# Row halves for the products with C, one fixed PSUM tile, and the step-size sums issued later, in an adaLN Mamba-2 block

## The chip, the cores and the metric

The kernel runs on one core of one Trainium2 chip. A core has a matrix engine (TensorE, PE in the profile; its weight loads are PEld), a vector engine (VectorE, DVE), an activation engine (ScalarE, ACT), a general engine (GpSimd, POOL) and a queue engine that issues transfers (SyncE, SP). The metric is the device time of one execution in microseconds (us). Matrix products accumulate in PSUM, eight banks of 2 KB per partition; a bank holds 128 x 512 numbers of 32 bits. All numbers are float32, and TensorE makes such a product in two passes, which the profile counts as two instructions.

## The reference, cut to what matters

Four sequences of 512 tokens with 512 features go through a normalized Mamba-2 block and a feed-forward layer with binarized weights. Both are modulated and gated by a vector c.

```python
h = layernorm(x) * (1 + ca) + sa
xBCzA = einsum('bld,ed->ble', h, in_proj_w)     # 2048 conv channels, 1024 z, 64 step sizes
xBC = silu(conv1d(xBC, width 4) + bias)         # x: 1024, B: 8 x 64, C: 8 x 64
dt = softplus(A_log); x_in = x / dt
# chunks of 128 tokens, 64 heads of 16, 8 groups of 8 heads, state 64
Y_diag = einsum('bcshn,bczhn,bhcsz,bczhp->bcshp', C, B, exp(segsum(-dt)), x)
states = einsum('bcshn,bhcs,bcshp->bchpn', B, decay_to_end, x)   # and a scan over chunks
Y_off = einsum('bcshn,bchpn,bhcs->bcshp', C, states_before, exp(cumsum(-dt)))
y = (Y_diag + Y_off + D * x_in) * silu(z + z_bias)
x = x + ga * (y @ out_proj.T)
h = layernorm(x) * (1 + cb) + sb
x = x + gb * (h @ binarized(ffn).T + ffn_b)
```

## The kernel before

The 2048 tokens are worked in eight halves of 256 tokens (two halves per sequence). A half has two chunks of 128 tokens (c) and four pairs of groups (gp), so eight units (h, c, gp), 64 in all. Every chunk but a sequence's first reads a state (48 units), and every chunk but its last makes one for the next (48 units).

The loop at the end of the program goes unit by unit. In a step it issues the exponentials of the unit ahead (`stage1`), then the pieces of other work that the lists FRONT and the tails put into that step, then the products of the step's own unit (`stage2`), and the loads of the decay sums for the unit after the next (`stage0`). A scheduler then sets each engine's order from the order of the program, priorities and its own estimate of when operands are there. A tile pool gives each tile a buffer; a tile that finds none free waits for the last reader of the oldest one.

FRONT spreads the work on half h over the eight steps of half h-1: load and normalize x, transpose it (`f_hT`), the step sizes (`f_dt`), then pairs of 128-channel projections for B, C and x in the order B0, C0, x0, x1, B1, C1, x2, x3, and z behind them. A pair (`conv_pair`, L367 to L391) is: four accumulating matmuls per tile into a PSUM buffer "mm" (names pp_B, pp_C, pp_x), a scaled copy on ScalarE (L379), three multiply-adds on VectorE per tile for the convolution (L383), one tanh on ScalarE (L387), and one last multiply on VectorE (L391). For C the last multiply is two, over 64 partitions each: group 0 of a pair goes to partitions 0 to 63 and the first 256 columns of each zeroed block `cd`, group 1 to partitions 64 to 127 and the other columns. So `cd` is block-diagonal, and one full-array matmul of 256 columns serves both groups of a pair.

B and x are then transposed to tokens by TensorE (L399, pt_bt and pt_xt, four transposes each) into PSUM buffers "tr", and copied by ScalarE (L418, L428). `f_dt` makes the 128 x 128 step sizes on VectorE, and behind them products with triangular matrices (pe L330 and L331, pc L344), exponentials and copies of them (sh L346, es), transposes (pn L353, pr L359), and three writes to DRAM (sums_d, e_d, r_d), from which later loads spread the values over partitions.

For a unit, `stage1` multiplies B with C (pg L509, masked into gm on VectorE L511), takes 16 exponentials on ScalarE (L516, 128 x 128 each) and multiplies them with gm (L519, twice 128 x 1024). `stage2` makes state times C (L543, 48 units), then 16 heads as column strips (L549): eight strips for each group r, of 32 output columns each, four side by side on the array, two accumulated. VectorE adds the two (L557, L558, or L561 in first chunks), GpSimd adds the skip term and multiplies with z (L559, L562). Products with B transposed (pst L574) update the state (L579, L584).

The tail of a chunk is the output projection (po L606), a layer norm, four transposes (ph L621), the feed-forward product (pf L634) and the output. PSUM is divided as: mm four banks, tr two, g one (pg), y one (py).

## Time and profile before

| what | before |
|---|---|
| time, median of three runs | 829.75 us (828.38 to 831.42) |
| profiled execution, its own time | 828.1 us |
| its span | 826.4 us |
| granted TensorE clock, mean | 0.980 |
| TensorE busy | 773.7 us, 5008 matmul passes |
| VectorE, ScalarE, GpSimd busy | 647.4, 529.2, 258.2 us |
| exponentials L516 | 1024, 313.8 us on ScalarE |
| decay products L519 | 128, 168.4 us on VectorE |
| writes of cd L391 | 32, 29.0 us on VectorE |
| products pg L509 and py L543 | 128 and 96 passes, 43.8 and 28.9 us busy on TensorE |

Of the page, the first part gives each engine's busy time, and the second cuts the span into 40 slices with the busy share in tenths. Matmuls are pipelined and overlap in the records, so the sum of their durations is more than the time they take; the time that one takes is better read from the start of one to the start of the next. The view of waits lists what an engine stood still for: the waiting instruction's tile and line, what it waited for, the total, how often and the longest.

### The profile page before, as it was taken

The numbers are of one execution on the slowest core, as the hardware profiler recorded it, in microseconds if no ns is written. First come the engines' busy times: TensorE is split into PE (matmuls) and PEld (weight loads), VectorE is DVE, ScalarE is ACT, GpSimd is POOL, SyncE is SP. The second block draws the span as 40 slices with busy tenths as digits, with TensorE's granted clock in tenths as the row PEclk, the third lists the DMA queues.
The fourth block names the chain that finished last, engine by engine and source line by source line (L and its number), as shares of the span: only waits on it lengthen the run. The fifth ranks groups of instructions, "written<-read, shape, count | busy, mean of one in ns | idle before, by whom it ended". The sixth has DMA issues, their size and how long they took to land. (4 is left out here: it accounts for less than half of the span.)

```text
span 826.4 us, 14794 instructions
## 1 busy us (share of the span) xinstructions
PE 773.7 (94%) x5008; PEld 531.7 (64%) x5008; DVE 647.4 (78%) x1249; ACT 529.2 (64%) x1510; POOL 258.2 (31%) x293
## 2 busy tenths in 40 slices
PE   5979889999999999999999999999999999999875
PEld 0853657767667767667667767667667766667431
DVE  3688779995899669995899669996899768995742
ACT  0455485677667778577767678476758687676640
POOL 5020312353223412353223412253213521353431
PEclk9979999999999999999999999999999999999986
DMA  8856542525344372425444272344434382343620
GB/s 297 324 136 199 148 103 68 136 62 137 94 116 127 87 180 68 129 70 128 103 112 133 74 190 68 104 94 104 128 101 113 91 204 52 113 103 90 147 58 13
DMA packets 120139, 99.26 MB, mean 120 GB/s; under 512 B 73976, under 2 KB 98552, under 8 KB 120064
## 3 DMA queue, kind: packets, MB, share of 16 engines
q1 hardware_dynamic: 120064, 98.32, 44.9%
q8 instruction: 40, 0.66, 0.4%
q14 instruction: 35, 0.29, 0.1%
HBM read 92.50 MB, written 5.79 MB: 119 GB/s over the span
## 5 line engine op out<-in xcount | busy, mean ns | idle before, releaser
L516 ACT ACTIVATE decay<-decay,st 128x128 f32<-128x128 f32 x1024 | 313.8, 390 | 39.5 <-DMA decay<-sums_d 39.0
L519 DVE SCALAR_TENSOR_TENSOR decay<-decay,gm 128x1024 f32<-128x1024 f32 x128 | 168.4, 1322 | 11.4 <-ACT decay L516 10.6
L367 PE MATMUL pp_x<-hT,win 128*128 128x259 f32 x512 | 124.5, 393 | 3.4 <-DVE u_B L383 3.4
L606 PE MATMUL po<-wout,z 128*128 128x512 f32 x256 | 122.0, 615 | 5.3 <-POOL z L562 5.3
L367 PE MATMUL pp_z<-hT,win 128*128 128x256 f32 x512 | 115.1, 379 | 0.0
L367 PEld LDWEIGHTS pp_x<-hT,win 128*128 128x128 f32 x512 | 95.6, 193 | 23.0 <-issue 7.7
L367 PEld LDWEIGHTS pp_z<-hT,win 128*128 128x128 f32 x512 | 95.4, 189 | 15.7 <-issue 3.3
L549 PE MATMUL py<-decay,xpad 128*32 128x128 f32 x2048 | 81.8, 280 | 6.6 <-DVE decay L519 5.4
L383 DVE SCALAR_TENSOR_TENSOR u_x<-pp_x,cw,u_x 128x256 f32<-128x256 f32 x192 | 81.8, 476 | 2.2 <-ACT u_x L379 1.7
L442 POOL TENSOR_TENSOR xs<-u_x,rr 128x512 f32<-128x512 f32 x32 | 47.2, 1474 | 112.7 <-DVE u_x L391 68.1
L606 PEld LDWEIGHTS po<-wout,z 128*128 128x128 f32 x256 | 47.2, 194 | 51.6 <-issue 44.1
L549 PEld LDWEIGHTS py<-decay,xpad 128*32 128x32 f32 x2048 | 54.1, 111 | 36.0 <-issue 23.8
L569 POOL TENSOR_TENSOR xd<-xpad,ed 128x256 f32<-128x256 f32 x48 | 35.2, 732 | 131.4 <-PE pst L574 101.8
L562 POOL TENSOR_TENSOR z<-yt,z 128x256 f32<-128x256 f32 x64 | 66.7, 1042 | 30.4 <-DVE yt L561 18.9
L559 POOL TENSOR_TENSOR yt<-yt,xs 128x256 f32<-128x256 f32 x48 | 38.9, 811 | 111.1 <-DVE yt L558 110.9
L634 PE MATMUL pf<-bwT,h 128*128 128x512 f32 x128 | 63.5, 636 | 6.6 <-DVE u_x L383 5.8
L367 PE MATMUL pp_B<-hT,win 128*128 128x259 f32 x256 | 60.6, 382 | 0.0
L367 PE MATMUL pp_C<-hT,win 128*128 128x259 f32 x256 | 58.9, 381 | 0.0
L623 ACT ACTIVATE h<-ph,modT 128x128 f32<-128x128 f32 x64 | 24.5, 456 | 48.7 <-PE ph L621 48.7
L451 ACT ACTIVATE uz<-pp_z,zb 128x256 f32<-128x256 f32 x64 | 26.9, 466 | 43.7 <-PE pp_z L367 41.7
L367 PEld LDWEIGHTS pp_B<-hT,win 128*128 128x128 f32 x256 | 47.5, 190 | 11.2 <-issue 4.3
L367 PEld LDWEIGHTS pp_C<-hT,win 128*128 128x128 f32 x256 | 48.4, 190 | 7.4
(129 smaller groups left out, 1083.3 us busy)
## 6 DMA issues: line engine op xcount, KB each, us to landing
decay<-sums_d SPq DMA_DIRECT2D x128, 256.0 KB
decay<-sums_d SPq DMA_DIRECT2D x128, 128.0 KB
rr<-r_d SPq DMA_DIRECT2D x64, 128.0 KB
wm<-in_w_mod SPq DMA_DIRECT2D x24, 256.0 KB
e<-e_d SPq DMA_DIRECT2D x96, 64.0 KB
x<-in_x SPq DMA_DIRECT2D x16, 256.0 KB
win<-in_w_inT SPq DMA_DIRECT2D x4, 1024.0 KB
xr<-in_x SPq DMA_DIRECT2D x16, 256.0 KB
```

The source lines that it names most:

```text
L367: mm(pm, win[:, k, col : col + P], H[h]["hT"][:, k, lo:], start=(k == 0), stop=(k == NK - 1))
L383: nc.vector.scalar_tensor_tensor(u[:, j, :], pm[:, k : k + T], cw[:, t, k : k + 1], u[:, j, :], ALU.mult, ALU.add)
L442: nc.gpsimd.tensor_tensor(xs, xc, rr, ALU.mult)
L451: nc.scalar.activation(u[:, q, :], pm[:, q, :], AF.Identity, bias=zb[:, 2 * j + q : 2 * j + q + 1], scale=0.5)
L516: nc.scalar.activation(ets[r][:, i, :], ets[r][:, i, :], AF.Exp, bias=H[h]["st"][:, hd : hd + 1])
L519: nc.vector.scalar_tensor_tensor(ets[r], ets[r], 1.0, bc_mid(gm[:, r, :], HPG), ALU.min, ALU.mult)
L549: mm(py[32 * j : 32 * j + 32, 0, r, :], xp[:, r * 2 * P + 32 * i : r * 2 * P + 32 * i + 32], ets[r][:, i, :], start=(q == 0), stop=(q == 1))
L559: nc.gpsimd.tensor_add(t, t, xs)
L562: nc.gpsimd.tensor_mul(zg, t, zg)
L569: nc.gpsimd.tensor_tensor(xd, xg, by_head(H[h]["ed"][:, hd0 : hd0 + HPP]), ALU.mult)
L606: mm(po, H[h]["z"][g // 2][:, g % 2, c * CH : (c + 1) * CH], wout[:, g, :], start=(g == 0), stop=(g == NKI - 1))
L634: mm(pf, h2[:, k, :], bwT[:, k, :], start=(k == 0), stop=(k == NK - 1))
```

## The change

C is kept once, as a tile of 128 partitions and two blocks of 256 tokens, with no zeros; its last multiply is one instruction over 128 partitions. The two groups of a pair lie on partitions 0 to 63 and 64 to 127, and B times C and state times C become two matmuls each, one on the upper and one on the lower half of the array's rows, of 128 columns.

The outputs with C, the strips and the state update go to one fixed PSUM tile `gy` of twelve runs of 128 columns (three banks): runs 0 and 1, or 5 and 6 for odd gp, hold a unit's strips, 3 and 4 its state output, 8 and 7 B times C, 9 and 10 the state update. All other PSUM tiles, the transposes of B and x and the step-size products among them, share five "mm" banks.

The new function `glued` issues the first of a list of products as it comes, and the others right behind it with high priority. It is used for the eight strips of one group, and for state times C of a unit with B times C of the unit two ahead. `stage0` and `stage1` of a unit are now issued two units ahead, behind `stage2` of the current one.

`f_dt` ends with the step sizes; all that followed (pe, pc, sh, es, pn, st, pr, rh and the three writes) is `f_sums`, which stands behind the first pairs of projections B0 and C0 and is issued after the last matmul of C0. The pools u, th and rr have one buffer more each (3, 2, 2).

```diff
-    ps = ctx.enter_context(tc.tile_pool(name="ps", bufs=4, space=PSUM))
+    ps = ctx.enter_context(tc.tile_pool(name="ps", bufs=5, space=PSUM))
-    cds = []
-    for i in range(3):
-        cd = keep.tile([P, 2, 2, T], F32, name=f"cd{i}")
-        nc.gpsimd.memset(cd, 0.0)
-        cds.append(cd)
+    bgy = ctx.enter_context(tc.tile_pool(name="bgy", bufs=1, space=PSUM))
+    gy = bgy.tile([P, 12, CH], F32, name="gy")
...
+    def f_sums(h):
+        W = 2 * NH
+        ndt, drdt = H[h]["ndt"], H[h]["drdt"]
+        with tc.issue_after(H[h]["last"]):
+            f_sums_products(h, W, ndt, drdt)
...
-        pt = ps.tile([P, 2, 2, P], F32, tag="tr", bufs=2, name=f"pt_{name}")
+        pt = ps.tile([P, 2, 2, P], F32, tag="mm", name=f"pt_{name}")
...
-        cd = cds[(2 * h + q) % 3]
-        conv_pair(
-            h, (DI + NG * NS) // P + 2 * q, f"C{q}",
-            [(cd[r * NS : (r + 1) * NS, :, r, :], slice(r * NS, (r + 1) * NS)) for r in range(2)],
-        )
-        H[h]["C"][q] = cd
+        t = wk.tile([P, 2, T], F32, tag="C", name=f"C_{h}_{q}", bufs=3)
+        conv_pair(h, (DI + NG * NS) // P + 2 * q, f"C{q}", t)
+        H[h]["C"][q] = t
...
+    def glued(products):
+        first = products[0]()
+        with tc.issue_after(first.ins), tc.high_priority(offset=1000):
+            for product in products[1:]:
+                product()
+
+    def by_rows(places, h, c, gp, stationary):
+        return [
+            partial(
+                mm, gy[:, places[r], :], stationary[part],
+                H[h]["C"][gp // 2][part, gp % 2, c * CH : (c + 1) * CH], start=True, stop=True,
+            )
+            for r, part in enumerate((slice(0, NS), slice(NS, P)))
+        ]
+
+    def state_out(h, c, gp):
+        k = (h % HPB) * 2 + c
+        return by_rows((3, 4), h, c, gp, states[h // HPB, k][:, gp, :]) if k > 0 else []
+
+    def b_times_c(h, c, gp):
+        return by_rows((8, 7), h, c, gp, H[h]["B"][gp // 2][:, gp % 2, c * CH : (c + 1) * CH])
...
-        pg = ps.tile([P, 2, CH], F32, tag="g", name=f"pg_{n}", bufs=1)
-        mm(pg, H[h]["B"][gp // 2][:, gp % 2, c * CH : (c + 1) * CH], c_pair(h, c, gp), start=True, stop=True)
-        nc.vector.tensor_mul(gm, pg, bc_mid(upto, 2))
+        nc.vector.tensor_mul(gm, gy[:, 7:9, :], bc_mid(upto, 2))
...
-        py = ps.tile([P, 2, 2, CH], F32, tag="y", name=f"py_{n}", bufs=1)
-        if k > 0:
-            mm(py[:, 1], states[b, k][:, gp, :], c_pair(h, c, gp), start=True, stop=True)
+        lo = 5 * (gp % 2)
+        py = gy[:, lo : lo + 2, :]
...
-            pst = ps.tile([P, P], F32, tag="tr", bufs=2, name=f"pst_{n}")
+            pst = gy[:, 9 + (c * NP + gp) % 2, :]
...
-        (4, f_B, (0,)), (4, f_C, (0,)), (4, f_Bt, (0,)),
+        (4, f_B, (0,)), (4, f_C, (0,)), (4, f_sums, ()), (4, f_Bt, (0,)),
...
+        elif step < len(units):
+            products = state_out(*units[step])
+            for unit in new:
+                products += b_times_c(*unit)
+            if products:
+                glued(products)
+            stage2(*units[step])
+            for unit in new:
+                stage0(*unit)
+                stage1(*unit)
```

More of the change, by code (lines that the diff above doesn't have):

```diff
@@ L1 @@
 from contextlib import ExitStack
+from functools import partial
 import numpy as np
@@ L187, in mod_cols @@
         nc.vector.tensor_scalar(row, pg, 1.0 if t6 in (1, 4) else 0.0, None, ALU.add)
-        pm = ps.tile([P, NK, B], F32, tag="tr", bufs=2, name=f"pm{t6}")
+        pm = ps.tile([P, NK, B], F32, tag="mm", name=f"pm{t6}")
         for dt in range(NK):
@@ L206, in gates_out @@
         grow = wk.tile([B, 3, DM], F32, tag="gates", name="grow", bufs=1)
-        brow = wk.tile([B, DM], F32, tag="th", name="brow", bufs=1)
+        brow = wk.tile([B, DM], F32, tag="th", name="brow")
         nc.sync.dma_start(brow, ffn_b.partition_broadcast(B))
@@ L301, in small @@
             return wk.tile([P, W], F32, tag=tag, name=f"{tag}_{h}", bufs=bufs)
-        pa = ps.tile([P, W], F32, tag="tr", bufs=2, name=f"pa_{h}")
+        pa = ps.tile([P, W], F32, tag="mm", name=f"pa_{h}")
         for c in range(2):
@@ L327, in f_dt, with f_sums_products @@
         )
-        pe = ps.tile([P, 2, W], F32, tag="tr", bufs=2, name=f"pe_{h}")
+        H[h].update(ndt=ndt, drdt=drdt)
+    def f_sums(h):
[3 more added lines that the diff above has]
+            f_sums_products(h, W, ndt, drdt)
+    def f_sums_products(h, W, ndt, drdt):
+        pe = ps.tile([P, 2, W], F32, tag="mm", name=f"pe_{h}")
         mm(pe[:, 0, :], after, ndt, start=True, stop=True)
@@ L340, in f_dt @@
             )
-        pc = ps.tile([NH, 2, 2, CH], F32, tag="tr", bufs=2, name=f"pc_{h}")
+        pc = ps.tile([NH, 2, 2, CH], F32, tag="mm", name=f"pc_{h}")
         for c in range(2):
@@ L350, in f_dt @@
         nc.sync.dma_start(e_d[h], es)
-        pn = ps.tile([P, W], F32, tag="tr", bufs=2, name=f"pn_{h}")
+        pn = ps.tile([P, W], F32, tag="mm", name=f"pn_{h}")
         for c in range(2):
             nc.tensor.transpose(pn[:, c * NH : (c + 1) * NH], sh[:, c, :], ident[:NH, :NH])
-        st = small("st", 2)
+        st = wk.tile([P, W], F32, tag="st", name=f"st_{h}")
         nc.vector.tensor_scalar(st, pn, -1.0, None, ALU.mult)
-        pr = ps.tile([NH, 2, CH], F32, tag="tr", bufs=2, name=f"pr_{h}")
+        pr = ps.tile([NH, 2, CH], F32, tag="mm", name=f"pr_{h}")
         for c in range(2):
@@ L366, in proj @@
         for k in range(NK):
-            mm(pm, win[:, k, col : col + P], H[h]["hT"][:, k, lo:], start=(k == 0), stop=(k == NK - 1))
+            last = mm(pm, win[:, k, col : col + P], H[h]["hT"][:, k, lo:], start=(k == 0), stop=(k == NK - 1))
+        return last.ins
     def conv_pair(h, t0, name, dst=None):
-        u = wk.tile([P, 2, T], F32, tag="u", name=f"u_{name}_{h}", bufs=2)
+        u = wk.tile([P, 2, T], F32, tag="u", name=f"u_{name}_{h}", bufs=3)
         for j in range(2):
@@ L377, in conv_pair @@
             pm = ps.tile([P, KS - 1 + T], F32, tag="mm", name=f"pp_{name}{j}_{h}")
-            proj(pm, h, t * P, 0)
+            H[h]["last"] = proj(pm, h, t * P, 0)
             nc.scalar.activation(
@@ L385, in conv_pair @@
                 )
-        th = wk.tile([P, 2, T], F32, tag="th", name=f"th_{name}_{h}", bufs=1)
+        th = wk.tile([P, 2, T], F32, tag="th", name=f"th_{name}_{h}")
         nc.scalar.activation(th, u, AF.Tanh)
-        if dst is None:
-            dst = [(u, slice(0, P))]
-        for d, r in dst:
-            nc.vector.scalar_tensor_tensor(d, th[r], 1.0, u[r], ALU.add, ALU.mult)
+        nc.vector.scalar_tensor_tensor(u if dst is None else dst, th, 1.0, u, ALU.add, ALU.mult)
         return u
     def to_tokens(src, name):
-        pt = ps.tile([P, 2, 2, P], F32, tag="tr", bufs=2, name=f"pt_{name}")
+        pt = ps.tile([P, 2, 2, P], F32, tag="mm", name=f"pt_{name}")
         for c in range(2):
@@ L403, in f_B @@
         t = wk.tile([P, 2, T], F32, tag="B", name=f"B_{h}_{q}", bufs=3)
-        conv_pair(h, DI // P + 2 * q, f"B{q}", [(t, slice(0, P))])
+        conv_pair(h, DI // P + 2 * q, f"B{q}", t)
         H[h]["B"][q] = t
     def f_C(h, q):
-        cd = cds[(2 * h + q) % 3]
-        conv_pair(
-            h, (DI + NG * NS) // P + 2 * q, f"C{q}",
-            [(cd[r * NS : (r + 1) * NS, :, r, :], slice(r * NS, (r + 1) * NS)) for r in range(2)],
-        )
-        H[h]["C"][q] = cd
+        t = wk.tile([P, 2, T], F32, tag="C", name=f"C_{h}_{q}", bufs=3)
+        conv_pair(h, (DI + NG * NS) // P + 2 * q, f"C{q}", t)
+        H[h]["C"][q] = t
     def f_Bt(h, q):
@@ L432, in f_xt @@
         H[h]["xt"][j] = xp
-        rr = wk.tile([P, 2, T], F32, tag="rr", name=f"rr_{h}_{j}", bufs=1)
+        rr = wk.tile([P, 2, T], F32, tag="rr", name=f"rr_{h}_{j}")
         for r in range(2):
@@ L448, in f_z @@
             proj(pm[:, q, :], h, NCONV + (2 * j + q) * P, KS - 1)
-        u = wk.tile([P, 2, T], F32, tag="u", name=f"uz_{h}_{j}", bufs=2)
+        u = wk.tile([P, 2, T], F32, tag="u", name=f"uz_{h}_{j}", bufs=3)
         for q in range(2):
@@ L453, in f_z @@
             )
-        th = wk.tile([P, 2, T], F32, tag="th", name=f"thz_{h}_{j}", bufs=1)
+        th = wk.tile([P, 2, T], F32, tag="th", name=f"thz_{h}_{j}")
         nc.scalar.activation(th, u, AF.Tanh)
@@ L495, in stage0 @@
         U0[h, c, gp] = (ets, e)
-    def c_pair(h, c, gp):
-        return H[h]["C"][gp // 2][:, gp % 2, :, c * CH : (c + 1) * CH]
+    def glued(products):
[16 more added lines that the diff above has]
+        return by_rows((8, 7), h, c, gp, H[h]["B"][gp // 2][:, gp % 2, c * CH : (c + 1) * CH])
     def stage1(h, c, gp):
@@ L519, in stage1 @@
             nc.vector.scalar_tensor_tensor(
-                ets[r], ets[r], 1.0, bc_mid(gm[:, r, :], HPG), ALU.min, ALU.mult
+                ets[r], ets[r], 1.0, bc_mid(gm[:, 1 - r, :], HPG), ALU.min, ALU.mult
             )
@@ L539, in by_head @@
             return v.rearrange("p (j q) -> p j q", q=2).unsqueeze(3).to_broadcast([P, HPG, 2, HD])
-        py = ps.tile([P, 2, 2, CH], F32, tag="y", name=f"py_{n}", bufs=1)
-        if k > 0:
-            mm(py[:, 1], states[b, k][:, gp, :], c_pair(h, c, gp), start=True, stop=True)
+        lo = 5 * (gp % 2)
+        py = gy[:, lo : lo + 2, :]
         for r in range(2):
-            for q in range(2):
-                for j in range(HPG // 2):
-                    i = 2 * j + q
-                    mm(py[32 * j : 32 * j + 32, 0, r, :], xp[:, r * 2 * P + 32 * i : r * 2 * P + 32 * i + 32],
-                       ets[r][:, i, :], start=(q == 0), stop=(q == 1))
+            glued([
+                partial(
+                    mm, py[32 * j : 32 * j + 32, r, :],
+                    xp[:, r * 2 * P + 32 * (2 * j + q) : r * 2 * P + 32 * (2 * j + q) + 32],
+                    ets[r][:, 2 * j + q, :], start=(q == 0), stop=(q == 1),
+                )
+                for q in range(2) for j in range(HPG // 2)
+            ])
         cs = slice(c * CH, (c + 1) * CH)
@@ L556, in stage2 @@
         if k > 0:
-            nc.vector.tensor_mul(t, py[:, 1], e)
-            nc.vector.tensor_add(t, py[:, 0], t)
+            nc.vector.tensor_mul(t, gy[:, 3:5, :], e)
+            nc.vector.tensor_add(t, py, t)
             nc.gpsimd.tensor_add(t, t, xs)
         else:
-            nc.vector.tensor_add(t, py[:, 0], xs)
+            nc.vector.tensor_add(t, py, xs)
         nc.gpsimd.tensor_mul(zg, t, zg)
@@ L676, in adaln_mamba_block @@
     for step in range(-1, max(steps) + 1):
-        ahead = step + 1 < len(units)
-        late = step < 0 or step % NU == NU - 1
-        if ahead and not late:
-            stage1(*units[step + 1])
         for f, args in steps.get(step, []):
             f(*args)
+        new = units[step + 2 : step + 3] if step >= 0 else units[0:2]
         if step < 0:
-            stage0(*units[0])
-        if 0 <= step < len(units):
+            for unit in new:
+                glued(b_times_c(*unit))
+                stage0(*unit)
[6 more added lines that the diff above has]
+                glued(products)
             stage2(*units[step])
-        if ahead and late:
-            stage1(*units[step + 1])
-        if step + 2 < len(units):
-            stage0(*units[step + 2])
+            for unit in new:
+                stage0(*unit)
+                stage1(*unit)
 _OUT = ((B, L, DM), np.float32)
```

## The prediction, made before the changed kernel ran

> **What bounds the kernel now.** I read the page's busy times and slices first, then TensorE's waits, then windows of 10 us, then the timeline around single projections.

> ```profile
> PE 773.7 (94%) x5008; PEld 531.7 (64%) x5008; DVE 647.4 (78%) x1249; ACT 529.2 (64%) x1510; POOL 258.2 (31%) x293
> PE   5979889999999999999999999999999999999875
> DVE  3688779995899669995899669996899768995742
> ```

> TensorE is the bound from the eighth slice to the 37th. VectorE reaches 9 tenths only in stretches, once per half of 256 tokens.

> ```profile
> engine line waited for: us in total, times, longest us
> PE pf L634 <- DVE u_x L383: 5.8, 3, 1.9
> PE pe L330 <- DVE ndt L322: 3.9, 4, 1.2
> PE pt_bt L399 <- DVE B L391: 1.8, 4, 0.7
> PE py L543 <- DVE yt L558: 1.2, 1, 1.2
> ```

> TensorE's waits in the steady part are few. They name VectorE.

> ```profile
> core 0: us, PE busy (x) PEld busy (x) DVE busy (x) ACT busy (x) POOL busy (x), PEclk, DMA share, GB/s
> 340.00:350.00 10.00, 10.00 (x78) 8.04 (x77) 10.00 (x21) 5.99 (x15) 2.25 (x2) 1.00 0.47 137
> 350.00:360.00 10.00, 10.00 (x73) 7.46 (x72) 9.76 (x24) 8.39 (x24) 6.27 (x9) 1.00 0.42 89
> 380.00:390.00 10.00, 10.00 (x89) 6.83 (x91) 7.45 (x10) 8.34 (x27) 3.05 (x3) 1.00 0.53 130
> ```

> While the next half's projections run (first two windows), TensorE and VectorE are both full; elsewhere TensorE alone is. So a reader of a projection stays unseen only because TensorE has other work in front of what needs it:

> ```profile
> 350.62 4.76 PE L367 MATMUL pp_x<-hT,win 128*128 128x259 f32 x21
> 351.92 0.56 ACT L379 ACTIVATE u_x<-pp_x,cb,cw 128x256 f32<-128x256 f32 x1 [1.19 <-PE pp_x L367]
> 355.16 0.62 ACT L387 ACTIVATE th_x<-u_x 128x512 f32<-128x512 f32 x1
> 355.82 0.69 DVE L391 SCALAR_TENSOR_TENSOR u_x<-th_x,u_x 128x512 f32<-128x512 f32 x1 [0.20 <-ACT th_x L387]
> 356.73 0.66 PE L399 MATMUL pt_xt<-ident,u_x 128*128 128x128 f32 x4
> ```

> The pair x2 of half 3 ends at 351.9. Its first reader (ScalarE) starts then, and the chain's last step on VectorE ends at 356.5, 4.6 us later. The four transposes start at 356.73, and TensorE lost almost nothing, since pp_x3, the state product and a row of strips stood between.

> **The change part by part.**

> The products. Around one unit, before:

> ```profile
> 425.57 0.59 PE L543 MATMUL py<-cd,S 128*128 128x256 f32 x2
> 426.09 1.08 PE L549 MATMUL py<-decay,xpad 128*32 128x128 f32 x32
> 427.10 0.70 PE L509 MATMUL pg<-cd,B 128*128 128x256 f32 x2
> 427.64 0.59 PE L634 MATMUL pf<-bwT,h 128*128 128x512 f32 x1
> ```

> Start to start, a 256-column pass takes 217 ns, a 128-column pass 110, and four column strips together 110. Entering the strips costs 310 instead of 217 (+93); leaving them 202 instead of 109 (+93), and the first full pass behind takes 320 instead of 217 (+104). The 64 L509 and 48 L543 products, two passes each, are 112 x 2 x 217 ns = 48.6 us, and 4.4 us of first-pass surcharges lie on full-array work that goes: -53 us. In their place stand 224 products on row halves, of two 128-column passes. No row of this trace shows two row halves side by side. If they run together as the column strips do: 224 x 110 ns = 24.6 us, and 12.9 us for entering and leaving: +37.5. Strips: they are cut into 104 stretches before (pn, pr and pst stand among them) and 86 after: 92.9 to 86.8 us, -6. Counting every matmul of both instruction orders by these prices (307 mode changes before, 348 after) gives 749.7 and 727.8 us: **-22 us**. If the halves run one after the other, another 24.6 us is due: +2.7. I take -22, by the nearest row (the strips, which share the array), and keep +2.7 as an end.

> [...]

> VectorE: 32 writes of cd (905 ns, 29.0 us) become 16 of 128x512 (u_x's and B's rows: 842 and 750 ns), 13 us: -16 us, two per half. VectorE doesn't end the half, so this is worth nothing by itself; it goes into the lag below. GpSimd loses three memsets of 2.7 us at the start, beside weight loads: nothing.

> The transposes. They move from a PSUM pool of their own into the five "mm" banks, and in the new order stand sooner behind their pair. TensorE work between a pair's end and its transposes, counted with the prices above, in us per half: xt0 8.1-8.9 before, 1.8-3.8 after; xt1 7.7-8.6, then 4.0-4.8; bt1 5.5-7.2, then 4.2-5.3; xt2 4.7-6.8, then 1.2-2.8; xt3 9.3-10.4, then 6.9; bt0 8.7-11.4, then 6.2-7.1. After xt0's pair now come one row group and two strip rows, and pp_x1, which used to cover it, is behind it; xt2 likewise. Over before's pairs, the time from a pair's end to its last VectorE step has a minimum of 4.2 and a median of 7.3 us (bare work: 0.56 + 3 x 0.40 + 0.63 + 0.69 = 3.1). At the minimum xt0 and xt2 each stall (4.2 + 0.15 for the signal) - 2 = 2.4 us: 4.9 per half, 34 us over seven halves. At the other end I walked half 4's new orders on ScalarE and VectorE with the row durations: between the x2 pair and its tanh ScalarE has eight exponentials (2.45 us), VectorE two decay products (1.22 each), yt, gm and S: xt2 stalls 4.75, xt0 2.4, xt1 0.2, and pn 3.4, since the copy of sh now stands behind some ten convolution steps on VectorE, where pn waited for nothing before. 10.8 per half, 75 us. It can't be below nothing: no transpose starts before its data. I take 7.5 per half, **+52 us**, between the two, because VectorE is full in these stretches but catches up while TensorE waits.

> Old stalls. pe (3.9), pf (5.8) and pt_bt (1.8) could go, since VectorE is later relieved and there are more buffers: 0 to -11.5, taken **-9**. What would be late next is the transposes above.

> The step-size sums behind the first projections: pe, pc, pn, pr, their ScalarE and VectorE readers and three DMA writes on SP. The sums are read by the decay loads of the next half's first unit, some three units (about 30 us) on, so the later SP issues cost nothing in the steady part; if that margin went, the exponentials (L516) would start late. In half 0 nothing covers it: pe follows pp_C01 at some 32 us and ndt is there at 36.3, 4.4 us idle, and xt0 and xt1 stall some 3 each: 11 us by 62 us into the span against 5.5 before, **+5** (3 to 8).

> New waits of the glued row group: it waits for gm of the unit before and for yt L557's reading of the state columns, with a whole row of strips queued behind it. The only such wait in the rows is py L543 on yt, once, 1.2 us; gm is made a unit earlier. 0 to 5, taken **+1**. Two units ahead instead of one, u, th and rr with another buffer: they take waits from ScalarE and GpSimd, which aren't the bound: nothing.

> Sum against the profiled execution's own 828.1 us (span 826.4 and 1.7 around it; 1.65 below the median 829.75): 828.1 - 22 + 52 - 9 + 5 + 1 = 855.1, and 856.8 at the median's level: **856**.

> **The rivals.**

> Faster, one mechanism: the lag shrinks to its bare 3.1 us, because VectorE has two us less per half and pauses with TensorE. Then xt0 and xt2 stall 1.1 each, 2 us per half, 16 in all: 828.1 - 22 - 9 + 16 + 3 + 1.65 = 818; with no stall at all 802. It decides where the stalls stay below some 4 us per half. For it: VectorE's share falls in the windows beyond 370 us. Against: no pair of before came below 4.2, and the x2 pair's 4.6 was among the shortest.

> Row halves one after the other: +24.6, some of which stands in front of the transposes and fills their stalls (0.4 per half): 856 + 25 - 3 = 878. For it: no row shows them side by side. Against: strips.

> Shortest lags everywhere: 856 - 18 = 838, the forecast's own lower end.

> **How the numbers follow.** Some 0.3% (2.5 us) can be told from no change. Forecast, with stalls of 34 to 75 us: 0.60, its own range 838 to 880. Faster rival: 0.23. Row halves not together: 0.12. Between 826 and 838, the stalls near 20 us: 0.05. The range that leaves out under 2 in 10 reaches into both: 814 to 884. Faster 0.23, same 0.03, slower 0.74.

> **What would show it.** Row halves: starts of the 64x128 matmuls in pairs some 6 ns apart (strips' spacing), pairs 110 ns apart; else 110 each. Transposes: new waits of TensorE on VectorE's last step for u_x (pt_xt), 2 to 5 us, fourteen or more, and pn on sh. VectorE's total near 631 us; PE's share of the span below 90%. Wrong if pt_xt waits under 1 us on average or the pairs of later halves end in under 4 us.

## The result and the profile after

The changed kernel takes 936.1 us (median of four runs, 930.7 to 937.8), the kernel before 830.6 us beside it: a ratio of 1.126 (95% interval 1.120 to 1.132). The forecast was 856 us, with a range of 814 to 884: the direction was right, the size was not. The profiled execution took 930.74 us, its span is 928.9.

The page of the changed kernel, first and second part, gives busy times and slices:

```profile
PE 791.7 (85%) x5232; PEld 547.9 (59%) x5232; DVE 633.0 (68%) x1233; ACT 533.7 (57%) x1510; POOL 239.5 (26%) x290
PE   4768788889978998979977998979978998989775
DVE  2567758775877569775878559775778559774652
PEclk9879989999989999999979999989989999999977
```

TensorE is busy for 85% of the span instead of 94%, and no other engine is full. The clock row dips all along. That of the kernel before dips at the start and the end only (one stretch of 3.4 us in the middle, at 520 us, is too short to show):

```profile
PEclk9979999999999999999999999999999999999986
```

The waits of TensorE (total, times, longest):

```profile
PE pt_xt L409 <- DVE u_x L401: 31.3, 18, 4.5
PE pn L365 <- DVE sh L358: 17.9, 7, 2.9
PE gy L602 <- DVE yt L586: 12.8, 8, 2.9
PE gy L506 <- DVE gm L537: 10.5, 13, 3.7
PE pe L342 <- DVE ndt L324: 8.4, 5, 4.6
PE gy L602 <- DVE mv_a L259: 7.2, 2, 3.6
PE gy L602 <- DVE yt L589: 5.1, 3, 3.5
PE pt_xt L409 <- DVE mv_a L259: 4.0, 1, 4.0
```

L409 are the transposes of x (35.3 us in all), L365 the transposes of the sums, L602 the state update's product pst (25.1 us: it now waits for its own unit's yt, which is read from the same tile gy), L506 the first of a glued row group, which waits for gm.

One such wait, by the timeline (start, length, and in brackets the idle time before it):

```profile
503.66 0.60 PE L379 MATMUL pp_x<-hT,win 128*128 128x259 f32 x2
504.30 0.56 ACT L392 ACTIVATE u_x<-pp_x,cb,cw 128x256 f32<-128x256 f32 x1 [0.61 <-PE pp_x L379]
504.65 1.22 DVE L545 SCALAR_TENSOR_TENSOR decay<-decay,gm 128x1024 f32<-128x1024 f32 x1
504.76 2.44 ACT L542 ACTIVATE decay<-decay,st 128x128 f32<-128x128 f32 x8
507.35 1.21 DVE L545 SCALAR_TENSOR_TENSOR decay<-decay,gm 128x1024 f32<-128x1024 f32 x1
509.05 0.63 ACT L400 ACTIVATE th_x<-u_x 128x512 f32<-128x512 f32 x1 [1.85 <-DVE u_x L396]
509.72 0.69 DVE L401 SCALAR_TENSOR_TENSOR u_x<-th_x,u_x 128x512 f32<-128x512 f32 x1
510.46 1.12 PE L409 MATMUL pt_xt<-ident,u_x 128*128 128x128 f32 x4 [4.55 <-DVE u_x L401]
511.37 4.64 PE L379 MATMUL pp_x<-hT,win 128*128 128x259 f32 x16
```

The x2 pair ends at 504.2; its chain has eight exponentials and two decay products in its way, as the prediction had walked it, and its transposes start at 510.46, with TensorE idle for 4.55 us (forecast for this place: 4.75). The last line shows what the prediction had no term for: the sixteen projection passes behind the wait take 4.48 us start to start, 280 ns each instead of 217. The windows around it:

```profile
470.00:480.00 10.00, 6.80 (x61) 5.40 (x59) 7.58 (x17) 8.26 (x24) 1.46 (x2) 0.84 0.33 90
480.00:490.00 10.00, 10.00 (x28) 7.02 (x28) 5.47 (x10) 6.38 (x19) 3.25 (x4) 0.70 0.51 122
500.00:510.00 10.00, 5.92 (x68) 4.69 (x60) 9.97 (x22) 6.60 (x18) 1.63 (x3) 1.00 0.47 124
510.00:520.00 10.00, 9.54 (x30) 6.56 (x31) 6.93 (x13) 6.33 (x20) 3.61 (x4) 0.83 0.09 23
```

The number behind the busy times is the granted clock. Behind the waits it is 0.84, 0.70 and 0.83: the record of the clock has stretches at 0.5, mostly of 3.4 or 6.8 us, 28 of them here, 6 before. From 480 to 490 TensorE is busy throughout, while VectorE and ScalarE are busy for 5.47 and 6.38 us of the ten: it is TensorE at its slower clock that holds the kernel there.

The row halves, by the timeline of the same place:

```profile
504.19 0.37 PE L506 MATMUL gy<-C,S 64*128 64x128 f32 x1
504.20 0.37 PE L509 MATMUL gy<-C,S 64*128 64x128 f32 x1
504.40 0.27 PE L506 MATMUL gy<-C,S 64*128 64x128 f32 x1
504.41 0.27 PE L509 MATMUL gy<-C,S 64*128 64x128 f32 x1
504.51 0.39 PE L509 MATMUL gy<-C,B 64*128 64x128 f32 x4
504.83 0.30 PE L506 MATMUL gy<-decay,xpad 128*32 128x128 f32 x1
```

The upper and the lower half start 6 to 8 ns apart in the trace (the view rounds to 10 ns), the second pair some 0.21 us behind the first and each later one some 110 ns behind the one before: they run together. A whole row group (state times C, and B times C) takes from 504.19 to 504.83, 0.64 us, where the two full-array products took 0.52 + 0.54 before.

**Where the time went.** For each run I split the span into TensorE's idle time between its first and last matmul, its busy time, and of that the part lost to the clock (busy time in stretches at clock 0.5, times 0.5); what is left is TensorE's work at full clock. The split is that of the one profiled execution of each kernel; the changed kernel's was its fastest, 930.7 us. The start (8 to 9 us) and the end (4.4) hardly differ.

| kernel | median us | ratio to before (95%) | idle | busy | lost to the clock | work at full clock |
|---|---|---|---|---|---|---|
| before | 830.6 | 1 | 38.8 | 773.7 | 12.4 | 761.3 |
| changed | 936.1 | 1.126 (1.120-1.132) | 124.8 | 791.7 | 53.5 | 738.2 |
| a_sums_back | 978.2 | 1.174 (1.163-1.185) | 147.9 | 815.1 | 78.6 | 736.5 |
| a_pst_mm | 921.4 | 1.106 (1.096-1.116) | 116.7 | 791.0 | 52.6 | 738.4 |
| a_xt_late | 867.7 | 1.041 (1.032-1.051) | 82.6 | 771.5 | 30.6 | 740.9 |
| a_all3 | 905.1 | 1.086 (1.075-1.097) | 110.1 | 782.7 | 45.6 | 737.1 |
| a_fill | 895.4 | 1.076 (1.065-1.086) | 79.3 | 802.1 | 29.0 | 773.1 |
| x_sh | 865.7 | 1.040 (1.024-1.056) | 84.2 | 769.9 | 26.7 | 743.2 |
| x_pn | 865.7 | 1.040 (1.029-1.050) | 83.6 | 768.1 | 25.8 | 742.3 |
| x_pn_bt | 856.0 | 1.028 (1.015-1.042) | 70.5 | 769.9 | 25.1 | 744.8 |
| a_pin_fill | 929.7 | 1.120 (1.116-1.123) | 96.9 | 820.1 | 46.0 | 774.1 |
| a_pin_fill2 | 922.4 | 1.111 (1.109-1.114) | 72.8 | 835.7 | 33.2 | 802.5 |
| b_share6 | 1006.2 | 1.212 (1.208-1.215) | 154.6 | 835.8 | 70.7 | 765.1 |
| a_tr | 854.4 | 1.029 (1.026-1.032) | 66.4 | 772.8 | 23.1 | 749.7 |
| a_gy2 | 805.6 | 0.972 (0.968-0.975) | 37.2 | 752.4 | 12.3 | 740.1 |
| gy2_sums_back | 808.9 | 0.974 (0.973-0.976) | 41.0 | 754.0 | 15.5 | 738.5 |
| gy2_noglue | 810.1 | 0.976 (0.975-0.978) | 38.9 | 758.0 | 12.9 | 745.1 |

From before to the changed kernel: idle +86.0, clock +41.1, work at full clock -23.1, start -1.4, together the 102.5 us of span, but for rounding. The last column is the check on the split: it is 736 to 750 for every kernel with row halves and no fillers, whatever its time, and 761 to 765 without row halves.

### The profile page after: what moved, and what is told of

The parts are those of the page before. It is cut to its first block, busy times and chain, and to the rows that moved or that the text cites. A ratio compares the mean times of both kernels' runs of the same rounds, so it can differ in the third digit from the quotient of the medians.

```text
span 928.9 us, 15115 instructions
## 1 busy us (share of the span) xinstructions
PE 791.7 (85%) x5232; PEld 547.9 (59%) x5232; DVE 633.0 (68%) x1233; ACT 533.7 (57%) x1510; POOL 239.5 (26%) x290
## 4 chain that ended last, share of the span: by engine, by line
PE 60%; DVE 21%; issue 7%; ACT 5%; DMA 4%; POOL 2%; SPq 1%; DVEq 0%; ACTq 0%; POOLq 0%
PE pp_z L379 12%; PE pp_x L379 11%; PE po L634 9%; PE pf L662 6%; PE gy L506 4%; PE pp_B L379 3%; DVE decay L545 3%; ACT decay L542 3%; DVE u_x L396 3%; DVE u_C L396 2%; PE gy L509 2%; PE pt_xt L409 2%; PE pp_C L379 2%; PE gy L602 2%; DVE u_B L396 2%
## 5 line engine op out<-in xcount | busy, mean ns | idle before, releaser
L545 DVE SCALAR_TENSOR_TENSOR decay<-decay,gm 128x1024 f32<-128x1024 f32 x128 | 164.1, 1284 | 40.9 <-ACT decay L542 36.8
L379 PE MATMUL pp_x<-hT,win 128*128 128x259 f32 x512 | 141.4, 435 | 0.0
L634 PE MATMUL po<-wout,z 128*128 128x512 f32 x256 | 121.6, 619 | 6.7 <-POOL z L590 6.7
L379 PEld LDWEIGHTS pp_x<-hT,win 128*128 128x128 f32 x512 | 112.7, 227 | 20.1 <-issue 0.7
L379 PE MATMUL pp_z<-hT,win 128*128 128x256 f32 x512 | 118.3, 385 | 0.0
L396 DVE SCALAR_TENSOR_TENSOR u_x<-pp_x,cw,u_x 128x256 f32<-128x256 f32 x192 | 88.3, 479 | 39.3 <-ACT u_x L392 36.9
L379 PEld LDWEIGHTS pp_z<-hT,win 128*128 128x128 f32 x512 | 96.8, 193 | 17.1 <-issue 4.4
L634 PEld LDWEIGHTS po<-wout,z 128*128 128x128 f32 x256 | 47.9, 195 | 57.2 <-issue 48.4
L509 PE MATMUL gy<-decay,xpad 128*32 128x128 f32 x1792 | 74.2, 279 | 0.0
L590 POOL TENSOR_TENSOR z<-yt,z 128x256 f32<-128x256 f32 x64 | 53.8, 841 | 59.5 <-DVE yt L589 42.5
L379 PE MATMUL pp_B<-hT,win 128*128 128x259 f32 x256 | 61.6, 392 | 0.0
L379 PE MATMUL pp_C<-hT,win 128*128 128x259 f32 x256 | 58.7, 381 | 0.0
L409 PE MATMUL pt_xt<-ident,u_x 128*128 128x128 f32 x128 | 26.4, 342 | 35.6 <-DVE u_x L401 31.3
L379 PEld LDWEIGHTS pp_B<-hT,win 128*128 128x128 f32 x256 | 49.3, 196 | 10.4 <-issue 3.3
L435 ACT COPY xpad<-pt_xt 128x512 f32<-128x512 f32 x32 | 18.6, 582 | 62.6 <-PE pt_xt L409 62.5
L396 DVE SCALAR_TENSOR_TENSOR u_B<-pp_B,cw,u_B 128x256 f32<-128x256 f32 x96 | 45.2, 473 | 11.8 <-ACT u_B L392 10.8
L392 ACT ACTIVATE u_x<-pp_x,cb,cw 128x256 f32<-128x256 f32 x64 | 35.7, 560 | 30.3 <-PE pp_x L379 30.0
```

Of the source, the lines that this page charges most:

```text
L379: last = mm(pm, win[:, k, col : col + P], H[h]["hT"][:, k, lo:], start=(k == 0), stop=(k == NK - 1))
L396: nc.vector.scalar_tensor_tensor(u[:, j, :], pm[:, k : k + T], cw[:, t, k : k + 1], u[:, j, :], ALU.mult, ALU.add)
L409: nc.tensor.transpose(pt[:, c, j, :], src[:, j, c * CH : (c + 1) * CH], ident)
L509: product()
L545: nc.vector.scalar_tensor_tensor(ets[r], ets[r], 1.0, bc_mid(gm[:, 1 - r, :], HPG), ALU.min, ALU.mult)
L590: nc.gpsimd.tensor_mul(zg, t, zg)
```

## The experiments

**Three waits, one by one.** The theory (A) was that TensorE's new waits add up, each with slower clock behind it; the rival (B) that a chain over VectorE and ScalarE is the bound and a wait that is taken away comes back at the next.

a_sums_back puts the sums ahead of the first projections again:

```diff
-        (1, load_x, ()), (2, f_norm, ()), (3, f_hT, ()), (3, f_dt, ()),
-        (4, f_B, (0,)), (4, f_C, (0,)), (4, f_sums, ()), (4, f_Bt, (0,)),
+        (1, load_x, ()), (2, f_norm, ()), (3, f_hT, ()), (3, f_dt, ()), (3, f_sums, ()),
+        (4, f_B, (0,)), (4, f_C, (0,)), (4, f_Bt, (0,)),
```

(and f_sums without its issue order.)

> The changed kernel with the step-size sums (pe, pc, sh, pn, pr) back behind the step sizes, ahead of the first projections. Theory A (TensorE's new waits add up, each with a slower clock behind it): the 17.9 us of pn waiting for sh and the extra 4 us of pe on ndt go, and some clock with them: 18 to 30 us below the changed kernel's 936, so 906 to 918. Theory B (a chain of VectorE and ScalarE is the bound, and a wait that is taken away comes back at the next): 928 to 940.

978 us, 42 slower than the changed kernel: both missed. pn hardly waits (1.0 us), but thirty row groups wait for gm (48.1 us):

```profile
PE gy L505 <- DVE gm L536: 48.1, 30, 4.2
PE pt_bt L408 <- DVE B L400: 15.6, 13, 2.8
PE pt_xt L408 <- DVE u_x L400: 14.2, 15, 4.0
```

In this kernel the later sums are a gain, not a part of the loss.

a_pst_mm gives pst a bank of its own:

```diff
-            pst = gy[:, 9 + (c * NP + gp) % 2, :]
+            pst = ps.tile([P, P], F32, tag="mm", name=f"pst_{n}")
```

> The changed kernel with the state update's product (pst) in an mm bank of its own instead of in the fixed tile gy, so that it no longer waits for the unit's own yt on VectorE. Theory A: its 25.1 us of waits go, with clock behind them: 900 to 914. Theory B: 925 to 940, the time turns up at the transposes.

921 us, 15 less: between the two. Of 25 us of waits at pst none is left, so they did come from reading and writing one tile (in the changed kernel all ten pst that stand directly behind strips wait; here, as before, such a pst starts at once); but gm takes 22.8 where it took 10.5, and pt_bt 5.9 where it took 1.5.

a_xt_late queues each x transpose behind the last projection of the next pair:

```diff
     def f_xt(h, j):
-        xc = H[h].pop("xc")
-        pt = to_tokens(xc, f"xt_{h}_{j}")
+        xc = H[h].pop(f"xc{j}")
+        with tc.issue_after(H[h]["last"]):
+            pt = to_tokens(xc, f"xt_{h}_{j}")
...
-        (5, f_x, (0,)), (5, f_xt, (0,)), (5, f_x, (1,)), (6, f_xt, (1,)),
-        (6, f_B, (1,)), (6, f_C, (1,)), (6, f_Bt, (1,)),
-        (7, f_x, (2,)), (7, f_xt, (2,)), (7, f_x, (3,)), (8, f_xt, (3,)), (8, f_z, (0,)),
+        (5, f_x, (0,)), (5, f_x, (1,)), (5, f_xt, (0,)),
+        (6, f_B, (1,)), (6, f_xt, (1,)), (6, f_C, (1,)), (6, f_Bt, (1,)),
+        (7, f_x, (2,)), (7, f_x, (3,)), (7, f_xt, (2,)), (8, f_xt, (3,)), (8, f_z, (0,)),
```

> The changed kernel with each x transpose queued behind the last projection of the pair after its own, so 4 to 10 us of TensorE work stand between instead of 1 to 5. Theory A: most of the 35 us that pt_xt waits go, and the clock's loss behind these waits, the longest of all: 885 to 910. Theory B: 920 to 940, with the wait at another VectorE result.

868 us, 68 less, more than A expected. The transposes of x wait 15.5 us instead of 35.3; and pst (25.1 to 2.7) and the row groups (10.5 to 2.9), which the edit does not touch, hardly wait any more; pt_bt rises from 1.5 to 8.0. The order of the transposes is the largest part of the loss.

> All three edits at once. Theory A: 25 + 22 + 31 us of waits less and 30 us or so of clock: 825 to 865, mean clock 0.965 or more. Theory B: above 895, less than half of the sum of waits.

905 us, in B's range: the three do not add up. With the sums ahead again, the strips wait for their decay products (36.3 us), which the other two edits cannot mend.

**Is it VectorE as a whole?** Two ways of taking pn's wait (19.0 us) from a_xt_late, and one more for the transposes of B1. x_sh puts the copy first:

```diff
-        nc.vector.tensor_copy(sh, pc[:, :, 0, :])
+        with tc.high_priority(offset=1000):
+            nc.vector.tensor_copy(sh, pc[:, :, 0, :])
```

x_pn makes pn, st, pr, rh and the last write a function of their own, f_sums2, issued after the last projection of x0:

```diff
-        (5, f_x, (0,)), (5, f_x, (1,)), (5, f_xt, (0,)),
+        (5, f_x, (0,)), (5, f_sums2, ()), (5, f_x, (1,)), (5, f_xt, (0,)),
```

x_pn_bt is x_pn with the transposes of B issued after the last projection so far, and those of B1 behind the pair x2:

```diff
-        (6, f_B, (1,)), (6, f_xt, (1,)), (6, f_C, (1,)), (6, f_Bt, (1,)),
-        (7, f_x, (2,)), (7, f_x, (3,)), (7, f_xt, (2,)), (8, f_xt, (3,)), (8, f_z, (0,)),
+        (6, f_B, (1,)), (6, f_xt, (1,)), (6, f_C, (1,)),
+        (7, f_x, (2,)), (7, f_Bt, (1,)), (7, f_x, (3,)), (7, f_xt, (2,)), (8, f_xt, (3,)), (8, f_z, (0,)),
```

> The kernel with the later x transposes (868 us) and the copy of sh put first on VectorE (high priority), so that pn need not wait for ten convolution steps. Waits add up: the 19.0 us of pn go, and some 5 us of clock: 842 to 852. Rival (VectorE is late as a whole in this stretch, so the next wait, at pt_bt or pt_xt, takes it): 858 to 868.

> The kernel with the later x transposes (868 us) and the transposes pn and pr queued behind the first x pair instead, 3.5 us later on TensorE; VectorE's order stays. Waits add up: 842 to 855, like putting the copy first. Rival: st comes later and the exponentials of the next half with it, 860 to 872.

> As x_pn, and the transposes of B1 queued one pair of projections later too. Of the 8.0 us that pt_bt waits some 5 go: 838 to 850. Rival: the wait moves to the x transposes, no more than 2 us below x_pn.

866, 866 and 856 us. For the first two the time is the rival's: in x_sh pn waits 1.5 us instead of 19.0, and the time turns up at the transposes (pt_xt 15.5 to 26.4, pt_bt 8.0 to 14.9); in x_pn it turns up at pt_bt (8.0 to 24.7). x_pn_bt lies between its two expectations.

```profile
PE pt_xt L410 <- DVE u_x L402: 26.4, 17, 2.6
PE pt_bt L410 <- DVE B L402: 14.9, 15, 2.5
PE pn L366 <- DVE sh L359: 1.5, 3, 0.5
```

A single late reader is not the cause then: once the worst order is mended, what waits is whatever stands next in front of VectorE's queue, and only more TensorE work between a pair and its reader (x_pn_bt) helps.

**The slower clock.** a_fill puts nine idle products into the transposes' own buffer ahead of the transposes of x0 and x2 (`fill` is 9 there and 0 elsewhere):

```diff
         pt = ps.tile([P, 2, 2, P], F32, tag="mm", name=f"pt_{name}")
+        for _ in range(fill):
+            mm(pt[:, 0, 0, :], ident, ones, start=True, stop=True)
```

> The changed kernel with nine idle products of 128 columns (some 2.0 us at full clock) written into the transposes' own PSUM buffer ahead of the transposes of x0 and x2, sixteen places, 32 us of TensorE work that nobody needs; the output is the same. Theory C (the slower clock behind a stall costs some 40 us of the loss): the idle time at these places shrinks by about 2 us each, the fillers themselves cost nothing there, and the clock behind them stays up: mean clock 0.95 or more, 905 to 928 us though TensorE has more work. Rival (the stall alone counts, the clock is a by-product): the fillers fill idle time and no more, 932 to 950.

895 us, below both ranges: 41 less than the changed kernel with 35 us more work, and a clock of 0.964. It does not settle the question: the scheduler gave the longer transposes another place (the first tile of the next pair went ahead of them), so the idle time fell by 45.5 us and not by the fillers' time alone.

So the order was taken out of the scheduler's hands: a list in the kernel chains all instructions of each engine in the changed kernel's own order, and the fillers stand only where TensorE stood idle, as many as fit (20 for the 4.55 us above). The second of the two kernels has them ahead of pe and pn too.

```diff
+    FILL = {'xt_0_0': 18, 'xt_0_1': 17, 'bt_0_1': 5, 'xt_1_1': 8, 'xt_1_2': 7, 'xt_2_0': 1, 'xt_2_2': 17,
+            'xt_3_2': 4, 'xt_4_0': 14, 'xt_4_2': 20, 'xt_5_2': 2, 'xt_6_0': 14, 'xt_6_1': 6, 'xt_6_2': 20}
...
+        idle = [mm(pt[:, 0, 0, :], ident, ones, start=True, stop=True).ins for _ in range(FILL.get(name, 0))]
...
+        for one, other in zip(chain, chain[1:]):
+            tc.add_manual_dep(
+                other, one.name,
+                mybir.DependencyInfo(mybir.DependencyClass.NoSync, mybir.DependencyReason.DATA), reason="pinned",
+            )
```

> The changed kernel with the order of every engine fixed as it was, and idle products of 128 columns put in front of those transposes at which TensorE stood still, in each place as many as fill the idle time seen there (153 products, 34 us at full clock, 35.3 us of waits). Theory C (the slower clock behind a stall costs some 41 us of PE work in all, about half of it behind these stalls): idle time falls by some 33 us, the fillers' own time replaces it, and 12 to 22 us of clock come back: 912 to 926, mean clock 0.95. Rival (clock no cause of its own): 932 to 942.

929.7 us, between the two theories: idle time falls by 27.9 us, and 7.5 us of clock come back, not 12 to 22. The time itself is not told from the changed kernel's (ratios 1.116 to 1.123 and 1.120 to 1.132). 24 stretches at clock 0.5 are left of 28, most of them behind waits at pst, pn and gm. With pe and pn filled as well:

> As the first fixed order with fillers, and TensorE's waits at pe and pn (some 26 us) filled too: 267 idle products, 59 us at full clock. Filling 28 us of idle time gave 7.5 us of clock back. If the slow clock follows TensorE's idle time: another 8 to 18 us of clock back, 908 to 924, although TensorE has 59 us more to do than in the changed kernel. Rival (the slow clock hangs on something else than idle time, or the filling itself adds as much as it saves): 926 to 942, PE work lost to the clock at 42 us or more.

922.4 us, 14 less than the changed kernel (8 less in the profiled executions, 922.5 and 930.7) though TensorE has 64 us more to do by the last column; the idle time is 52 us less, and 20.3 of the 41 us of clock are back. The slow clock follows idle time, at one fixed order of all engines; it is a loss of its own and not only a sign of waiting.

**What moved the transposes?** One edit in the kernel before makes its pools of four and two banks one of six (b_share6; pm, pa, pe, pc, pn, pr and pst change their tag as pt does):

```diff
-    ps = ctx.enter_context(tc.tile_pool(name="ps", bufs=4, space=PSUM))
+    ps = ctx.enter_context(tc.tile_pool(name="ps", bufs=6, space=PSUM))
...
-        pt = ps.tile([P, 2, 2, P], F32, tag="tr", bufs=2, name=f"pt_{name}")
+        pt = ps.tile([P, 2, 2, P], F32, tag="mm", name=f"pt_{name}")
```

> The kernel before with one edit: the two tr banks and the four mm banks become one pool of six, which the transposes and the step-size products share with the projections, as they share one in the changed kernel. In its order the transposes of x0 and x2 stand only 2 us of TensorE work behind their pair, as in the changed kernel. If the shared pool is the cause: transposes wait as in the changed kernel, 875 to 940. Rival (the order comes from the units two ahead, the glue or the later sums, and VectorE keeps up here): 825 to 845.

1006 us, 21% slower than before, and outside both expectations on the far side. Nothing but the pool is changed, and the TensorE work between a pair and its transposes falls from 8.1-8.9 to 2.0-2.2 us (xt0, from the second half on) and from 4.7-6.8 to 1.1-2.3 (xt2), as in the changed kernel. TensorE waits for many things that VectorE makes:

```profile
PE py L549 <- DVE decay L519: 39.6, 23, 3.8
PE pt_xt L399 <- DVE u_x L391: 29.1, 16, 3.2
PE pg L509 <- DVE gm L511: 16.8, 8, 3.4
PE py L543 <- DVE yt L558: 15.3, 10, 2.6
PE pt_bt L399 <- DVE B L391: 15.1, 12, 2.1
```

The transposes themselves wait 44.2 us of the 115.8 us that the idle time grew by. How much of the rest follows from their place, and how much from the new place of other work on TensorE, is not shown.

The opposite edit in the changed kernel makes its five banks three and two (a_tr; pm, pa, pe, pc, pn and pr go with pt):

```diff
-    ps = ctx.enter_context(tc.tile_pool(name="ps", bufs=5, space=PSUM))
+    ps = ctx.enter_context(tc.tile_pool(name="ps", bufs=3, space=PSUM))
...
-        pt = ps.tile([P, 2, 2, P], F32, tag="mm", name=f"pt_{name}")
+        pt = ps.tile([P, 2, 2, P], F32, tag="tr", bufs=2, name=f"pt_{name}")
```

> The changed kernel with its five mm banks split into three for the projections and two (tr) for transposes and step-size products, as before; all else as changed. The transposes then stand 5 to 9 us behind their pair. If the shared pool is the cause: 830 to 865 (three banks hold the projections back at times). Rival: above 900.

854 us, 82 less than the changed kernel, and the transposes of x wait 1.2 us. With three banks for the projections these wait now:

```profile
PE pp_C L379 <- DVE u_B L396: 14.6, 8, 3.9
PE pp_x L379 <- DVE u_x L396: 6.9, 7, 1.2
PE pp_x L379 <- DVE u_C L396: 6.4, 6, 2.9
```

So the shared pool is what moves the transposes. Why the scheduler places them so with one pool was not tried.

**A version that keeps the rest.** a_gy2 is the changed kernel with four mm and two tr banks (pst in tr), and gy in two banks:

```diff
-    ps = ctx.enter_context(tc.tile_pool(name="ps", bufs=5, space=PSUM))
+    ps = ctx.enter_context(tc.tile_pool(name="ps", bufs=4, space=PSUM))
...
-    gy = bgy.tile([P, 12, CH], F32, name="gy")
+    gy = bgy.tile([P, 8, CH], F32, name="gy")
...
-        return by_rows((8, 7), h, c, gp, H[h]["B"][gp // 2][:, gp % 2, c * CH : (c + 1) * CH])
+        return by_rows((2, 5), h, c, gp, H[h]["B"][gp // 2][:, gp % 2, c * CH : (c + 1) * CH])
...
-        nc.vector.tensor_mul(gm, gy[:, 7:9, :], bc_mid(upto, 2))
+        nc.vector.tensor_mul(gm, gy[:, 2:6:3, :], bc_mid(upto, 2))
...
-        lo = 5 * (gp % 2)
+        lo = 0
...
-            pst = gy[:, 9 + (c * NP + gp) % 2, :]
+            pst = ps.tile([P, P], F32, tag="tr", bufs=2, name=f"pst_{n}")
```

> The changed kernel with the kernel before's pools (four mm banks, two tr banks, in which pst is again), and gy in two banks instead of three: strips in runs 0 and 1 for every unit, B times C in 2 and 5, state output in 3 and 4. Row halves, glue, sums behind the first projections and units two ahead stay. TensorE's work at full clock is 23 us below before's; transposes stand 5 to 10 us behind their pair. If only the pool was wrong: 800 to 825, faster than before. Rival (VectorE bounds the stretches with the projections, so the gain can't be had there): 825 to 845.

805.6 us, 2.8% below the kernel before (ratio 0.972, 0.968 to 0.975), with the idle time and the lost clock of before and 21 us less work. Its page, the first lines of parts 1 and 2:

```profile
PE 752.4 (94%) x5232; PEld 518.1 (65%) x5232; DVE 626.0 (78%) x1233; ACT 526.8 (66%) x1510; POOL 242.2 (30%) x290
PE   4999799999999999999999999999999999999865
```

and the transposes of the x2 pair of half 3 in its timeline:

```profile
342.30 0.57 ACT L392 ACTIVATE u_x<-pp_x,cb,cw 128x256 f32<-128x256 f32 x1 [1.21 <-PE pp_x L379]
347.36 2.84 PE L634 MATMUL po<-wout,z 128*128 128x512 f32 x6
349.63 0.69 DVE L401 SCALAR_TENSOR_TENSOR u_x<-th_x,u_x 128x512 f32<-128x512 f32 x1
350.37 0.65 PE L409 MATMUL pt_xt<-ident,u_x 128*128 128x128 f32 x4 [0.17 <-DVE u_x L401]
```

The pair ends at 342.3 and its last step on VectorE at 350.32, 8.0 us later; but TensorE has pp_x3, a row group, strips and part of the output projection (po) in between, and stands idle for 0.17 us. The x2 pair of half 4, the one of the 4.55 us above, makes TensorE wait for nothing here (its transposes start at 441.97).

Two parts of the change, taken out of this version (the sums ahead again; the products of a list in the scheduler's own order):

> The 806 us kernel with the step-size sums back behind the step sizes, ahead of the first projections. If the later sums are worth something of their own: 810 to 825, pe waits for ndt again as before (3.9 us) and pn for sh. Rival (with the transposes covered it is all one): 801 to 809.

> The 806 us kernel without the glue: products of a list are issued by the scheduler's own order. By the prices of the trace of before, strips broken up cost about 0.3 us a piece; the order has about 3 us more TensorE work at full clock. If the glue carries part of the gain: 808 to 816. Rival: 803 to 808.

808.9 and 810.1 us. The later sums are not told from nothing here: the intervals (0.973 to 0.976 and 0.968 to 0.975) overlap, and waits of pe (4.4 us) come back as expected; those of pn do not. Without the glue TensorE's work at full clock is 745.1 us instead of 740.1, so some 5 of the 21 us are the glue's; the two intervals (0.975 to 0.978, 0.968 to 0.975) just touch.

## Why the prediction was wrong

**Products and strips, -22 us: right.** Work at full clock fell by 23.1 us in the changed kernel and by 21.2 in a_gy2; the row halves start some 7 ns apart. The rival of halves one after the other is out. A row group took 0.64 us, against 1.06 for the two full-array products before.

**Transposes, +52 us: right in size, in part by luck.** The waits at pt_xt (35.3) and pn (17.9) are 53.2 us, some 8 of them in half 0, which the +52 did not count: 6.5 us per later half, forecast 7.5. For half 4 the walk came out: 10.6 us, walked 10.8 (x2 4.55 and 4.75, xt0 3.2 and 2.4, pn 2.7 and 3.4). But the halves differ, which no step named: the transposes of x wait 21.6 us in halves 2, 4 and 6 and 5.7 in halves 1, 3, 5 and 7, and only seven of their nineteen waits reach 2 us, where fourteen were forecast. The middle between the two ends happened to fit the mean.

**New waits of the glued row group, +1 (0 to 5): the first step that failed.** Row groups waited 11.6 us, for gm and yt. And pst, which the step did not name, waited 25.1 for its own unit's yt, since both now lie in gy: 37 us in place of 1, far outside the ends given. a_pst_mm shows the tile to be the reason for pst's wait; a_xt_late shows that a better order hides most of both.

**Old stalls, -9: too much.** pf's 5.8 us went; pt_bt kept 1.5 of 1.8, and pe rose from 3.9 to 8.4, 4.6 of it in half 0, which the +5 for the start had named.

**The clock: the second step that failed, the largest, since the sum had no term for it.** 41.1 us more of TensorE work were lost to the clock than before. The trace of before had the rows for it: at half 0, behind waits of 2.6 and 2.9 us, the clock was 0.64 and 0.85 in the two windows from 50 to 70 us, and 3.5 us of work were lost.

```profile
PE py L549 <- DVE decay L519: 5.4, 4, 2.6
PE pp_x L367 <- DVE u_B L383: 3.4, 2, 2.9
50.00:60.00 10.00, 4.54 (x26) 3.10 (x25) 7.72 (x12) 5.69 (x19) 4.22 (x3) 0.64 0.47 117
60.00:70.00 10.00, 10.00 (x50) 6.83 (x50) 8.42 (x19) 9.09 (x25) 0.00 (x0) 0.85 0.40 94
```

At the rate that the changed kernel showed afterwards (41.1 of clock to 86.0 of idle time, 0.48), the 52 us of new waits would have brought 25 us more: 881, just inside the upper end of the range.

**The account of the miss.** The profiled execution lies 75.6 us above the sum for it (930.7 and 855.1). 41.1 are the clock, and 37 are idle time beyond the forecast (86.0, where the four terms for waits make 49); products and start give back 2.5. The slips in the sum's own figures are small: 856.8 became 856, and twice 2.4 became 4.9.

**The faster rival** needed the stalls at the transposes below some 4 us per half; with pn they were 6.7 (53.2 over eight). The rival "shortest lags" is out as well. VectorE's forecast (631 us, measured 633.0) and TensorE's share below 90% (85%) came out.

The prediction saw that the transposes had lost their cover, and named the move into the shared banks and the new order side by side without saying which did it; b_share6 and a_tr show that sharing the pool is enough to do it, and that parting it undoes it.

## What to carry to other kernels

Compare the instruction order of the bound engine before and after an edit of pools, not only the code: merging two pools into one moved the transposes next to their producers, and by itself made the kernel before 21% slower. Price a new wait of TensorE at its length and something more for the clock behind it (0.48 us per us of added idle time in the changed kernel, 0.30 to 0.61 in the other slower kernels without fillers here), and look for tiles that are read and written in one piece by several users. When a large change loses, take its account apart (idle, clock, work at full clock): here the part that was meant to help did help, and the change with the old pools (a_gy2) was worth 2.8%.
